# Re-ordering a spline convolution layer: all distances of a turn first, the copies of the next turns earlier, the output add between the splines, and the last stores on two queues

## The chip, the core and the metric

The kernel runs on one core of a Trainium2 chip. A core has four compute engines[...]: TensorE (PE, matrix multiplications; PEld is its weight load), VectorE (DVE), ScalarE (ACT) and GpSimd (POOL). SyncE (SP) only issues DMAs here. Everything is fp32. Time is the device time of one execution in microseconds (us).

## The reference, cut to what matters

Four convolution layers run one after the other on x of shape (8 images, 16 channels, 128, 128), each as x = x + layer(group norm(x)). The change touches the last one, a layer of cubic B-splines:

```python
patches = _extract_patches(x, KSIZE, STRIDE, PAD)          # 3x3 neighbours of each point
bspl = _b_splines(patches, grid)                           # 8 spline values of each element
base_w = base_weight.sum(axis=2)
spl_w = (spline_weight * spline_scaler[..., None]).sum(axis=2)
out = jnp.einsum('bjhwn,ijn->bihw', jax.nn.silu(patches), base_w)
out = out + jnp.einsum('bjhwns,ijns->bihw', bspl, spl_w)
out = out + bias_weight[None, :, None, None]
...
x = x + _L3_conv_ref(_gn(x), ...)
```

So every element becomes eight spline values, these are convolved 3x3 down to 16 channels, a 3x3 convolution of silu(x) is added, then a bias and x itself.

## The kernel before

The stage is laid out in 32 **turns**. A turn (k, g) makes output rows 8k to 8k+7 of four images, those numbered 2q+g with q from 0 to 3; g alternates, so two turns in a row share k. x stays in SBUF, one partition for each image and channel. In the text, "image q" of a turn is the q-th of its four.

The splines of a turn, class `Splines`, take these steps. Its rows are split into two halves, h = 0 and 1, of four rows each (512 columns)[...].

- `spread(h)`: TensorE copies the 16 channels of each image onto 128 partitions (eight spline bases by 16 channels) by a matrix of zeros and ones, four PSUM tiles `far`, one an image (L1204). An fp32 matrix multiplication shows as two instructions in the trace. The pool holds six `far` tiles, so a spread needs two that the spread just before it used.
- `near(h, q)`: ScalarE turns one `far` tile into the scaled distance from the base's centre, `v` (L1149, `v<-far`). The tile `v` has four buffers and 1024 columns, both halves of one image.
- `clip(q)`: VectorE limits `v` to 6 (L1154) and the tiles `e` and `p`, two buffers each, are taken.
- `finish(q)`: ScalarE makes `e` and `p` from `v` (L1149, `e<-v` and `p<-v`), VectorE multiplies them into `p` (L1162, "the p step") and writes the spline values to a tile `s` (L1169, `put`, "the spline"). GpSimd copies the two rows that overlap from the `s` of two turns earlier (L1258). The twelve `s` tiles hold three turns.

The last two turns have seven new rows (896 columns) in place of eight. The first row of an image, `first_row`, is made apart, in the two first turns.

`convolve(t, lo, hi)` adds positions lo to hi-1 of fifteen to the accumulator `acc3` of turn t (L1322): twelve positions of splines and three of silu, each with four products (one for each image, in its own 32 columns of the array), eight instructions a position in the trace. `acc3` has two buffers.

`finish(t)` outside the class adds accumulator, bias and the residual (the tile `o`, L1335, four buffers), and stores it with eight DMAs. `residual(t)` loads `o` with eight DMAs from x (L1301). `silu(k)` serves two turns: ScalarE makes `sil` (one buffer, its edges set to zero by GpSimd at L1269 and L1270), and sixteen DMAs spread it to `four` (L1286, two buffers).

The order of work on VectorE, ScalarE and TensorE is the order of the calls: `in_turn` ties each instruction to the one before it on its engine. GpSimd and SyncE are ordered by a scheduler, roughly as the calls stand. Every buffer is guarded by semaphores that the framework places. Each DMA of SyncE also waits for the landing of the one eight places before it.

`make(t, conv, done)` is the turn: it makes the splines of turn `t` while turn `conv`, two before it, is convolved, and the output of turn `done`, one before `conv`, is finished. The lines of the profile lie in the functions below.

Of the kernel before, what the change touches and what calls it, by code (L numbers as in the profile page):

```python
# [21 lines left out]
NP = B // 2  # L22
# [78 lines left out]
def kernel(  # L101
# [20 lines left out]
    nc = tc.nc  # L122
# [22 lines left out]
    def lut(out_, in_, func, **kw):  # L145
        name = sets.get(func, str(func))
        last = phase["all"]
        if name != phase["name"]:
            phase.update(name=name, first=None, all=[])
            if name == "exp_ln":  # L150
                begin(nc.scalar.preload_act_table_set("natural_log_exp_and_others").ins, last)
        ins = nc.scalar.activation(out_, in_, func, **kw).ins  # L152
        if phase["first"] is None:
            begin(ins, last)
        else:
            tc.add_manual_dep(ins, phase["first"].name, order, reason="table set")
        phase["all"].append(ins)
        return ins
# [51 lines left out]
    def in_turn(engine, ins):  # L210

        if engine in chain:
            tc.add_manual_dep(ins, chain[engine].name, order, reason="in turn")
        chain[engine] = ins
        return ins
# [3 lines left out]
    for n in range(5):  # L219
        t = cpool.tile([BC, BC], F32, name=f"w1_{n}")  # L220
# [13 lines left out]
    with ExitStack() as l0:  # L234
        wp = l0.enter_context(tc.tile_pool(name="w0", bufs=1))
        with tc.tile_pool(name="x0", bufs=2) as xp:
            bn0 = xp.tile([BC, NCH, 6], F32, name="bn0", bufs=1)
            for j in range(8):
                t = xp.tile([BC, HW // 8], F32, name="xj")
# [102 lines left out]
        def work(name):  # L342
            return tmp.tile([128, 2, 512], F32, tag="work", name=name, bufs=11)
# [28 lines left out]
        class Variances:  # L372
# [19 lines left out]
            def finish(self):  # L392
                w, pv = work("r0"), banks[:, 0]
                r0, sq = w[:, 0], w[:, 1]
                lut(r0, pv, AF.Ln, bias=eps_t, scale=-2.0)
                lut(r0, r0, AF.Exp, scale=-0.5)
                nc.scalar.activation(sq, r0, AF.Square)
                nc.vector.scalar_tensor_tensor(pv, pv, -0.5 * EPS, sq, op0=ALU.add, op1=ALU.mult)
                r = act.tile([128, 512], F32, name="rstd", bufs=2)
                nc.vector.scalar_tensor_tensor(r, pv, 1.5, r0, op0=ALU.add, op1=ALU.mult)  # L400
                return r
# [254 lines left out]
        for n in range(-2, NCH + 3):  # L656
            if n + 2 < NCH:
                steps[n + 2] = Step(4 * (n + 2))
            done = steps.pop(n - 2, None)
# [6 lines left out]
            def put(i, f, *a):  # L666
                between[i].append(lambda: f(*a))
# [458 lines left out]
    with ExitStack() as l3:  # L1126
# [24 lines left out]
        def curve(v, width):  # L1151

            v = v[:, :width]
            in_turn("dve3", nc.vector.tensor_scalar_min(v, v, 6.0).ins)  # L1154
            e = tmp.tile([128, 1024], F32, name="e")[:, :width]
            p = tmp.tile([128, 1024], F32, name="p")[:, :width]
            yield
            act(e, v, AF.Square, scale=1.0 / 3.0, bias=minus)
            act(p, v, AF.Prelu, scale=1.0 / 3.0, bias=minus, alpha=-3.0)
            in_turn(  # L1160
                "dve3",
                nc.vector.scalar_tensor_tensor(  # L1162
                    p, p, 3.0, e, op0=ALU.subtract, op1=ALU.mult
                ).ins,
            )
            yield v, p
# [8 lines left out]
        turns = [(k, g) for k in range(H // 8) for g in range(2)]  # L1175
# [14 lines left out]
        def of(t, q):  # L1190
            return tiles[4 * (t % 3) + q]
# [4 lines left out]
        def spread_rows(t, lo, n):  # L1196

            g = turns[t][1]
            out_ = []
            for q in range(NP):  # L1200
                p = ps.tile([128, 512], F32, name="far", bufs=6)
                in_turn(
                    "pe3",
                    mm(  # L1204
                        p[:, : n * W],
                        copy[32 * q : 32 * q + 32, g],
                        x[32 * q : 32 * q + 32, lo * W : (lo + n) * W],
                        start=True,
                        stop=True,
                    ).ins,  # L1210
                )
                out_.append(p[:, : n * W])
            return out_

        def distance(v, p, t, q):
            b = 2 * q + turns[t][1]
            act(v, p, AF.Abs, scale=fac[:, 0, b : b + 1], bias=fac[:, 1, b : b + 1])

        def first_row(t):
            ps_ = spread_rows(t, 0, 1)  # L1220
            v = tmp.tile([128, 1024], F32, name="v", bufs=4)
            for q, p in enumerate(ps_):
                distance(v[:, q * W : (q + 1) * W], p, t, q)
            c = curve(v, 512)
            next(c)
            v, p = next(c)
            for q in range(NP):
                cols = bass.ts(q, W)
                put(of(t, q)[:, 1, 1 : 1 + W], v[:, cols], p[:, cols])
                nc.gpsimd.tensor_copy(of(t, q)[:, 0, :], edge)  # L1230
# [77 lines left out]
        def convolve(t, lo, hi):  # L1308

            k, g = turns[t]  # L1310
            if lo == 0:
                accs[t] = ps.tile([128, 4, W], F32, name="acc3")
            for n in range(lo, hi):
                s, dw = divmod(n, 3)
                for q in range(NP):
                    if s < 4:
                        w_, v = wspl[:, s, dw], of(t, q)[:, s : s + 7 : 2, dw : dw + W]
                    else:
                        w_, v = wbase[:, g, dw], sils[k][:, q, :, dw : dw + W]
                    in_turn(  # L1320
                        "pe3",
                        mm(  # L1322
                            accs[t][32 * q : 32 * q + 32],
                            w_.rearrange("p a f -> p (a f)"),
                            v,
                            start=(n == 0),
                            stop=(n == 14),
                            skip_group_check=True,
                        ).ins,
                    )  # L1330

        def finish(t):
            k, g = turns[t]
            o = outs.pop(t)
            ins = nc.vector.scalar_tensor_tensor(  # L1335
                o, accs.pop(t), bias3, o, op0=ALU.add, op1=ALU.add
            ).ins
            in_turn("dve3", ins)
            for q in range(NP):
                for p in range(2):  # L1340
                    lo = 32 * q + 16 * p
                    nc.sync.dma_start(
                        out[2 * q + g, :, 8 * k : 8 * k + 8, :].rearrange(
                            "f (i p) w -> f p i w", p=2
                        )[:, p],
                        o[lo : lo + 16],
                    )

        def make(t, conv, done):

            sp = Splines(t) if t < len(turns) else None
            if conv is not None:
                convolve(conv, 0, 2)
            if sp:
                if sp.k == 0:
                    first_row(t)
                sp.spread(0)
                for q in range(NP):
                    sp.near(0, q)
            if conv is not None:  # L1360
                convolve(conv, 2, 7)
            if sp:
                sp.spread(1)
                sp.near(1, 0)
                sp.clip(0)
                sp.near(1, 1)
                sp.clip(1)
                sp.finish(0)
                sp.near(1, 2)
                sp.clip(2)  # L1370
                sp.finish(1)
            if conv is not None:
                convolve(conv, 7, 15)
            if done is not None:
                finish(done)
            if sp:
                sp.near(1, 3)
                sp.clip(3)
                sp.finish(2)
                sp.finish(3)  # L1380

        silu(0)
        make(0, None, None)
        residual(0)
        make(1, None, None)
        for t in range(len(turns)):
            if t + 1 < len(turns):
                residual(t + 1)
            if t % 2 == 0 and t + 2 < len(turns):
                silu(t // 2 + 1)  # L1390
            make(t + 2, t, t - 1 if t else None)
        finish(len(turns) - 1)


# [71 lines left out]
```

## Time and profile before

| what | us |
|---|---|
| median of 3 runs | 11252.07 (11250.59 to 11255.03) |
| the profiled execution | 11250.13 |
| its span, first to last instruction | 11248.3 |
| the stage concerned, from the first `sil` memset | 10569.6 to 11248.3 |
| time from one turn's output add to the next, in the middle of the stage | 20.47 |
| one distance, 128x512 (ScalarE L1149) | 0.773 |
| one `e` and one `p`, 128x1024 (ScalarE L1149) | 1.146 and 1.137 |
| one p step and one spline, 128x1024 (VectorE L1162, L1169) | 1.220 and 1.225 |
| one limit, 128x1024 (VectorE L1154) | 0.689 |
| one output add, 128x512 (VectorE L1335) | 0.745 |
| one `sil`, 128x1280 (ScalarE L152) | 1.442 |

The profile is of one execution. A group of instructions is shown as line, engine, operation, tile written <- tiles read, shape and count, then busy time and mean, then the idle time of the engine just before them and what ended it. In the lines of waits, "A <- B" means that A's engine stood idle until B; the numbers are the total, the count and the longest. PEclk is the share of TensorE's full clock that was granted. Durations of two neighbouring instructions on one engine overlap a little, so the time from start to start is shorter than a duration.

Around this stage, the turns before the first convolution take from 10,578 to about 10,619 us, and the convolutions end at 11,241.6.

### The profile page before, as it was taken

The page shows a single profiled execution, that of the slowest core. Times are in us where ns is not written, and L with a number is a line of the kernel's source. Part 1 is how long each engine was busy: PE and PEld are TensorE (multiplying, and loading weights), DVE is VectorE, ACT ScalarE, POOL GpSimd, SP SyncE. Part 2 cuts the span into 40 slices and gives each one's busy share as a digit, 9 for nine tenths or more (in the row PEclk, how much of TensorE's full clock was granted, in tenths as well). Part 3 has the DMA queues.
Part 4 walks back from the last instruction along what each step waited for, and adds up shares of the span by engine and source line. Part 5 has one row for each costly group of instructions (what it writes and reads, how often), then busy time and mean ns, then how long its engine had stood idle before and what let it go on. Part 6 is the DMA issues. An engine that isn't in the chain of part 4 may idle for free.

```text
span 11248.3 us, 173864 instructions
## 1 busy us (share of the span) xinstructions
PE 8843.7 (79%) x72372; PEld 2092.2 (19%) x72372; DVE 9068.7 (81%) x6829; ACT 8780.2 (78%) x7107; POOL 4873.1 (43%) x2681
## 2 busy tenths in 40 slices
PE   5999999999986777777777777777777777777788
PEld 1222222222222111111111111111111111111122
DVE  3555555555555799999999999999999999999865
ACT  2555555555545799999999999999999999999876
POOL 3555555555553633333334333334334333343300
PEclk8999999999998899999999999999999999999899
DMA  1000000000003300000000000000000000000022
GB/s 47 13 15 15 12 13 15 15 13 13 14 6 94 119 7 7 13 7 7 8 12 7 7 13 7 7 13 7 7 13 7 7 13 7 7 7 7 20 54 50
DMA packets 189391, 203.91 MB, mean 18 GB/s; under 512 B 46777, under 2 KB 155449, under 8 KB 186553
## 3 DMA queue, kind: packets, MB, share of 16 engines
q1 hardware_dynamic: 180264, 190.81, 6.4%
q8 instruction: 569, 9.32, 0.3%
q10 hardware_dynamic: 8336, 1.97, 0.1%
q14 instruction: 222, 1.81, 0.1%
HBM read 107.15 MB, written 60.04 MB: 15 GB/s over the span
## 4 chain that ended last, share of the span: by engine, by line
DVE 44%; PE 31%; ACT 14%; issue 5%; POOL 2%; DMA 1%; SPq 1%; DVEq 0%; ACTq 0%; POOLq 0%
DVE t L1003 22%; PE banks L360 17%; DVE u L1009 14%; PE pn L971 10%; ACT t L992 9%; DVE y L518 2%; PE acc L1322 2%; ACT u L152 1%; POOL y L527 1%; DVE x L538 1%; ACT hid L152 1%; PE pd L971 1%; DMA yd<-y 1%; DVE x L630 1%; SPq L1286 1%
## 5 line engine op out<-in xcount | busy, mean ns | idle before, releaser
L971 PE MATMUL pn<-f,wa 32*64 32x512 f32 x18432 | 3413.7, 625 | 1711.6 <-DVE u L1009 1687.3
L1024 POOL TENSOR_TENSOR v<-t,u 128x1024 f32<-128x1024 f32 x1152 | 2739.8, 2378 | 4017.4 <-DVE t L1003 3871.3
L1009 DVE TENSOR_TENSOR u<-pn,u 128x1024 f32<-128x1024 f32 x2304 | 2713.7, 1219 | 117.7
L971 PE MATMUL pd<-f,wb 32*64 32x512 f32 x18432 | 2601.0, 626 | 161.1 <-ACT t L992 94.6
L1003 DVE SCALAR_TENSOR_TENSOR t<-t,u 128x2048 f32<-128x2048 f32 x1152 | 2630.6, 2283 | 33.9 <-ACT u L152 33.6
L992 ACT ACTIVATE t<-pd 128x1024 f32<-128x1024 f32 x2304 | 2338.4, 1015 | 311.2 <-PE pn L971 304.7
L152 ACT ACTIVATE u<-t 128x2048 f32<-128x2048 f32 x1152 | 2202.5, 1912 | 51.9 <-PE acc L1055 15.9
L152 ACT ACTIVATE u<-u 128x2048 f32<-128x2048 f32 x1152 | 2190.7, 1902 | 0.0
L971 PEld LDWEIGHTS pn<-f,wa 32*64 32x64 f32 x18432 | 750.0, 131 | 3775.4 <-DVE u L1009 3246.1
L1016 DVE SCALAR_TENSOR_TENSOR u<-t,u 128x1024 f32<-128x1024 f32 x1152 | 1418.5, 1231 | 37.9
L152 ACT ACTIVATE hid<-banks 128x1024 f32<-128x1024 f32 x576 | 571.8, 1023 | 1049.6 <-PE banks L360 1047.7
L1055 PE MATMUL acc<-u,const 128*32 128x512 f32 x9216 | 1257.2, 618 | 1.8 <-DVE u L1016 1.8
L527 POOL TENSOR_TENSOR y<-y 128x1536 f32<-128x1536 f32 x256 | 895.0, 3496 | 833.6 <-DVE y L518 833.6
L518 DVE TENSOR_TENSOR y<-banks,vp 128x1536 f32<-128x1536 f32 x384 | 673.0, 1753 | 274.8 <-PE banks L360 271.6
L544 ACT ACTIVATE sq<-x 128x1024 f32<-128x1024 f32 x384 | 398.0, 1054 | 412.3 <-DVE x L538 289.7
L470 POOL TENSOR_TENSOR pd<-q,kp 128x1536 f32<-128x1536 f32 (+1 forms) x256 | 694.0, 2737 | 7.6 <-PE banks L360 5.9
L971 PEld LDWEIGHTS pd<-f,wb 32*64 32x64 f32 x18432 | 514.5, 132 | 751.9 <-ACT t L992 690.7
L360 PE MATMUL banks<-att,const 32*128 32x512 f32 x2304 | 499.0, 669 | 173.7 <-DVE att L509 96.0
L360 PE MATMUL banks<-h,wfc 64*128 64x512 f32 (+1 forms) x3072 | 620.5, 632 | 14.5 <-DVE h L606 14.5
L1055 PE MATMUL acc<-v,const 128*32 128x512 f32 x4608 | 616.5, 606 | 0.2 <-POOL v L1024 0.2
L606 DVE TENSOR_TENSOR h<-banks,x 128x1024 f32<-128x1024 f32 x192 | 232.6, 1211 | 437.9 <-ACT hid L152 227.6
L1322 PE MATMUL acc<-s,wspl 128*32 128x512 f32 x3072 | 389.2, 650 | 92.5 <-DVE o L1335 92.5
(181 smaller groups left out, 7329.3 us busy)
## 6 DMA issues: line engine op xcount, KB each, us to landing
f<-yd SPq DMA_DIRECT2D x512, 101.6 KB
yd<-y SPq DMA_DIRECT2D x320, 130.0 KB
xin<-in_x SPq DMA_DIRECT2D x752, 32.0 KB
four<-sil SPq DMA_DIRECT2D x256, 65.0 KB
xj<-in_x SPq DMA_DIRECT2D x8, 1024.0 KB
xl<-in_x SPq DMA_DIRECT2D x32, 256.0 KB
x1d<-xl SPq DMA_DIRECT2D x32, 256.0 KB
x<-x1d SPq DMA_DIRECT2D x8, 1024.0 KB
```

The source lines that it names most:

```text
L152: ins = nc.scalar.activation(out_, in_, func, **kw).ins
L360: in_turn("pe", mm(*args, skip_group_check=True, **kw).ins)
L470: ins = nc.gpsimd.tensor_mul(t[:, :n].rearrange("p n (a b) -> p n a b", a=4), rows(self.q[d][:, k]).unsqueeze(1).to_broadcast([128, n, 4, W]),
L518: ins = nc.vector.tensor_mul(y.rearrange("p n (a b) -> p n a b", a=4), banks[:, 1:4].rearrange("p n (a b) -> p n a b", a=4), windows(v, j, 3),
L527: in_turn("pool", nc.gpsimd.tensor_add(self.y[k], self.y[k], y).ins)
L971: yield mm(p[64 * (u % 2) : 64 * (u % 2) + 64, u // 2], w[lo : lo + 32, q % 2, n].rearrange("p c f -> p (c f)"), fs[g * NP + q][lo : lo + ...
L992: in_turn("act", nc.scalar.activation(self.t[:, ab], self.pd.pop(ab), AF.Abs).ins)
L1003: ins = nc.vector.scalar_tensor_tensor(self.t, self.t, 1.0, self.u, op0=ALU.add, op1=ALU.mult).ins
L1009: ins = nc.vector.tensor_mul(self.u[:, ab], self.pn.pop(ab), self.u[:, ab]).ins
L1016: ins = nc.vector.scalar_tensor_tensor(r, self.t[:, :, 0], 2.0, r, op0=ALU.subtract, op1=ALU.mult).ins
L1024: ins = nc.gpsimd.tensor_mul(self.v, self.t[:, :, 1], self.u[:, :, 1]).ins
L1055: ins = mm(accs[k][32 * q : 32 * q + 32], gather[:, int(part == 1), g], (c.u[:, ab, 0], c.u[:, ab, 1], c.v[:, ab])[part], start=first, sto ...
```

## The change

`make` is split. `begin_turn(t)` starts the splines of a turn: the first row if there is one, `spread(0)` and `near(0, q)` of all four images. `make(sp, done)` then issues all second halves of the distances with their limits, and after them the four `finish(q)`, with the output add of turn `done` between images 1 and 2. `done` is now the turn just convolved, t, where it was t-1. The loop places the two spreads of turn t+2 after eight and after ten of the fifteen positions of turn t (before: after two and after seven). Turn 0 has an order of its own, since the splines of turn 1 are still being made in it. In the last turn, every second image's two stores are issued from ScalarE in place of SyncE.

```diff
             for q in range(NP):
+
+                eng = nc.scalar if t == len(turns) - 1 and q % 2 else nc.sync
                 for p in range(2):
                     lo = 32 * q + 16 * p
-                    nc.sync.dma_start(
+                    eng.dma_start(
...
-        def make(t, conv, done):
-
-            sp = Splines(t) if t < len(turns) else None
-            if conv is not None:
-                convolve(conv, 0, 2)
+        def begin_turn(t):
+
+            if t >= len(turns):
+                return None
+            sp = Splines(t)
+            if sp.k == 0:
+                first_row(t)
+            sp.spread(0)
+            for q in range(NP):
+                sp.near(0, q)
+            return sp
+
+        def make(sp, done):
+
             if sp:
-                if sp.k == 0:
-                    first_row(t)
-                sp.spread(0)
                 for q in range(NP):
-                    sp.near(0, q)
-            if conv is not None:
-                convolve(conv, 2, 7)
-            if sp:
-                sp.spread(1)
-                sp.near(1, 0)
-                sp.clip(0)
-                sp.near(1, 1)
-                sp.clip(1)
-                sp.finish(0)
-                sp.near(1, 2)
-                sp.clip(2)
-                sp.finish(1)
-            if conv is not None:
-                convolve(conv, 7, 15)
-            if done is not None:
+                    sp.near(1, q)
+                    sp.clip(q)
+                for q in range(NP):
+                    if q == 2 and done is not None:
+                        finish(done)
+                    sp.finish(q)
+            elif done is not None:
                 finish(done)
-            if sp:
-                sp.near(1, 3)
-                sp.clip(3)
-                sp.finish(2)
-                sp.finish(3)
 
         silu(0)
-        make(0, None, None)
+        sp = begin_turn(0)
+        sp.spread(1)
+        make(sp, None)
+        sp = begin_turn(1)
         residual(0)
-        make(1, None, None)
         for t in range(len(turns)):
             if t + 1 < len(turns):
                 residual(t + 1)
             if t % 2 == 0 and t + 2 < len(turns):
                 silu(t // 2 + 1)
-            make(t + 2, t, t - 1 if t else None)
-        finish(len(turns) - 1)
+            if t == 0:
+                convolve(t, 0, 2)
+                sp.spread(1)
+                make(sp, None)
+                convolve(t, 2, 8)
+            else:
+                convolve(t, 0, 8)
+            sp = begin_turn(t + 2)
+            convolve(t, 8, 10)
+            if sp:
+                sp.spread(1)
+            convolve(t, 10, 15)
+            make(sp, t)
```

## The prediction

> **What bounds the kernel now.** The edit lies in the last stage alone (span 10,569 to 11,248 us), so I read only that. First the waits of a stretch of ten turns there (10,900 to 11,104 us, 20.48 us a turn):
>
> ```profile
> POOL s L1258 <- PE acc L1322: 151.2, 10, 19.0
> DVE v L1154 <- ACT v L1149: 56.4, 10, 5.7
> ACT v L1149 <- PE far L1204: 40.8, 20, 2.7
> PE acc L1322 <- DVE o L1335: 32.4, 10, 3.2
> ```
>
> Columns: total us, times, longest. POOL's wait delays nobody; the other three form a ring. TensorE cannot open a turn until VectorE's `o` of the turn before has freed an accumulator (3.2 us each), ScalarE waits for TensorE's copies, VectorE for ScalarE. No engine is full. What each would need alone comes from the groups of the same stretch:
>
> ```profile
> L1169 DVE SCALAR_TENSOR_TENSOR s<-v,p 128x1024 f32<-128x1024 f32 x40 | 49.0, 1225 | 4.7
> L1162 DVE SCALAR_TENSOR_TENSOR p<-p,e 128x1024 f32<-128x1024 f32 x40 | 48.8, 1220 | 15.9 <-ACT p L1149 15.9
> L1154 DVE TENSOR_SCALAR v<-v 128x1024 f32<-128x1024 f32 x40 | 27.3, 689 | 56.4 <-ACT v L1149 56.4
> ...
> L1149 ACT ACTIVATE e<-v,minus 128x1024 f32<-128x1024 f32 x40 | 45.8, 1146 | 16.1 <-DVE v L1154 15.1
> ```
>
> VectorE: 49.0+48.8+27.3+7.5 (`o`) = 132.6 for ten turns, 13.3 a turn. ScalarE: 57.6+45.8+45.5+7.2 = 156.1, 15.6 by durations; starts overlap ends, so by start-to-start (0.67 a copy, 1.05 an `e` or `p`, 1.34 a `sil` every second turn) it is 8x0.67+8x1.05+0.67 = 14.4. Next, the granted clock in three stretches, the columns after the stretch being its length and the engines' busy times:
>
> ```profile
> 10971.88:10975.29 3.41, 3.41 (x16) 0.68 (x16) 3.31 (x4) 2.98 (x3) 0.00 (x0) 0.50 0.27 57
> 10975.29:10992.36 17.07, 13.84 (x128) 3.86 (x128) 9.46 (x11) 12.49 (x15) 1.68 (x6) 1.00 0.34 74
> 10992.36:10995.77 3.41, 3.41 (x16) 0.64 (x16) 3.31 (x4) 2.19 (x2) 0.00 (x0) 0.50 0.27 58
> ```
>
> After each stop for `o`, TensorE runs 3.41 us at half clock. Warm, four convolution instructions start every 0.431 us, so a turn's 120 take 12.93, its two `far` groups 1.07 each: 15.07 us. Last, the timeline of SyncE's DMA queue for two turns:
>
> ```profile
> 11012.65 3.64 SPq L1342 DMA_DIRECT2D out<-o  x8
> 11016.86 10.67 SPq L1286 DMA_DIRECT2D four<-sil  x16
> 11027.58 1.88 SPq L1301 DMA_DIRECT2D o<-x  x3
> 11033.12 3.63 SPq L1342 DMA_DIRECT2D out<-o  x8
> 11036.80 9.17 SPq L1301 DMA_DIRECT2D o<-x  x13
> ```
>
> 28.99 us in two turns of 40.96: idle for 12.
>
> [...] ScalarE idles 1.5 us for `e` ten times although the `sil` behind needs nothing of it. So an order of issue is an order of execution, and I may add start-to-start times. [...] at 10,591.15 the `p` step took 1.43 beside a GpSimd copy, against 1.22. [...]
>
> **The change, part by part.** Per engine the instructions stay the same; they are re-ordered, and four of 256 store DMAs go to ScalarE's queue.
>
> *Output add.* `finish(t)` moves from turn t+1 into turn t's own splines, behind image 1's. Accumulators are two, so turn t+1 needs the one that t-1 freed a turn earlier. TensorE's 3.24 us stop goes, and with it the cold window (16 instructions in 3.41 us instead of 1.72, so 1.7). What is late next? With TensorE free, 15.07 would be the turn, if nothing else were longer.
>
> *All distances first.* ScalarE's order is now near(0,0..3), near(1,0..3), then e, p for images 0 to 3. `v` has four buffers, one for each image, so near(0,3) of the next turn must wait for image 3's spline, the last VectorE step of this one, and all eight remaining distances and curves stand behind it. That closes a new ring. With near(0,3) at 0, from start-to-start times of the timeline: near(1,0) 0.67, near(1,3) 2.70, e0 3.36, p0 4.41, first `p` step 5.57 (1.16 after p0). VectorE then runs unbroken: four pairs of `p` step to spline (1.34), after images 0, 1 and 2 1.14, after `o` 0.66: 4x1.34+3x1.14+0.66 = 9.44 (the 1.14 behind image 1 leads to `o`, at 10.5), so image 3's spline starts at 15.01, lasts 1.23, and near(0,3) follows 0.04 later: **16.28 us**. Does anything inside wait longer? e and p have two buffers: e2 needs the first `p` step done (6.84, its turn 7.56), p3 needs spline 1 (10.66, its turn 10.71): no. `sil` runs 11.72 to 13.06, before near(0,3): hidden by this wait; without that cover it would cost 0.67 a turn.
>
> *Copies ahead.* spread(0) of turn t+2 goes behind 8 of 15 positions, spread(1) behind 10. The second one's images 2 and 3 wait for near(0,0) and near(0,1), at the latest 14.5; conv(t,10..15) and the next 8 positions are queued behind. They end 5 and 12 us later, `o` needs the first at 10.5 of the next round (26.8), so 7 us of slack. TensorE idles 1.2 us a turn here on average, 2.6 in a `sil` turn and none in the next. Should that turn it cold, 1.7 is lost against those 2.5 per pair of turns: still hidden.
>
> *Queues passed.* SyncE's blocks keep their order per pair: 8 stores, 16 `four`, 3 loads, 8 stores, 13 loads: 29 of now 32.6 us. A round's stores start at 11.3, `four` at 15.1, lands by 29, wanted by the memset and `sil` at 44.3. GpSimd's four copies (0.36 each) wait for a convolution that ends near 2.3 to 3.6 and are over by 5.1, before VectorE's two-input steps at 5.57; bound 0 to 1.4 us a turn, I take 0.
>
> *Prologue.* Turn 0: e0 moves from 10,585.92 to 10,587.1 behind four distances, but the curves then run unbroken: splines end 10,599.0 (before 10,599.5). Turn 1: its first row at 10,600.6, `sil`, near(1,0) 10,604.8, p0 10,608.5, last spline done 10,619.4 (before 10,618.8): +0.6.
>
> *End.* 28 rounds of 16.28 and one of 14.6 (the last two turns have 896 columns: 0.67+1.71+0.57+0.95+1.06, then 4x1.2+3x1.01+0.66, then 1.13): 10,619.4+455.8+14.6 = 11,089.8. Turn 31's last spline is done 14.6 later, 11,104.4; conv(30) ends about 11,104.6; conv(31) 12.93+0.5: 11,118.0. `o` 0.75. From there to the end before: 5.9 us, with eight issues of 0.46; two queues halve them, -1.8 (bounds 0 and -1.8): 11,122.9.
>
> **Sum.** I add 0.1 us a round for waits taken as exact: 11,125.8 span. The profiled execution took 11,250.13 for a span of 11,248.3, so 1.83 around it: 11,127.6. The median of the runs is 1.94 above that execution: 11,129.5, rounded **11,130 us**, 1.1% less. About 0.2%, 22 us, is what a measurement can tell from no change.
>
> **Rivals.**
> A (forecast): the `v` ring, 16.3 to 16.5: 11,122 to 11,140. Chance 0.72.
> B: a round of 17 to 17.8. The turn of before is exactly six clock windows (20.48); if TensorE's idle falls into one window it may settle at five, 17.07: 0.69x29 = 20 over the forecast's 16.38, 11,150. Or SyncE's DMAs, spaced by landings, stretch as traffic grows by a quarter: 29 to 35 per pair, the same figures. For: 2.6 of 3.41 us idle can be cold. Against: the slack above. 0.17.
> C: TensorE's own 15.07, if near(0,3)'s wait came earlier than I read: -1.3x29: 11,092. Against: `v` has four buffers in both kernels. 0.07.
> D, slower: `four`'s landing. `sil` stands ahead of all distances on ScalarE and waits for the last turn-pair's sixteen DMAs and a GpSimd memset; if they land more than 16 us (44.3-28.2) late, ScalarE stops, and with it VectorE, TensorE and the next stores. Past a round of 20.48 it loses: landing 16+8.3 = 24 us late per pair. A round of 22.5 would give 11,250+2x29 = 11,310. Nothing in the queue shows such a delay. 0.03.
> E: the stage is bound by something I do not see and stays: 11,250. 0.01.
> So faster 0.96, same 0.01, slower 0.03; range 11,110 to 11,160, which leaves out C, the upper part of B, and D.
>
> **What would show it.** Right: turns 16.3 apart; "PE acc <- DVE o" gone; ScalarE's L1149 `v` waiting some 1.1 to 2.5 us per turn for DVE `s` L1169; clock near 1.00 in the stage; SyncE idle about 3 us per pair; TensorE's waits moved to `far` <- ACT `v`. Wrong: turns of 17 us or more with SyncE never idle or a 0.50 clock each turn (B); 15.1 us with no ACT wait on DVE `s` (C); ACT `sil` waiting for DMA `four` (D).

## The result, and the profile after

| | before | after |
|---|---|---|
| median (range), us | 11251.33 (11248.15 to 11255.03), 4 runs | 11132.26 (11130.52 to 11134.61), 4 runs |
| ratio to before | | 0.9894, 95% interval 0.9881 to 0.9907 |
| span of the profiled execution | 11248.3 | 11132.8 |
| last stage, from its first distance to the end of the span | 669.9 | 551.1 |
| one output add to the next, mean over the middle of the stage | 20.35 | 16.45 |
| last output add (its start) to the end of the span | 6.72 | 5.36 |
| time at half clock from 10,625 us to the end of the span | 95.5 | 12.9 |

The kernel became 119 us, 1.1%, faster; the forecast was 11,130 us, 1.1%. In the profiled executions the last stage is 118.8 us shorter, and what runs ahead of it took 3.3 us longer. (A round is the time from one turn's output add to the next.) Some 29 rounds shorter by 3.90 make 113, the shorter end 1.4; the remaining 4 lie in the first and last turns.

The waits of ten turns of the kernel after come first (total us, times, longest us):

```profile
DVE v L1154 <- ACT v L1149: 16.0, 10, 1.6
DVE p L1162 <- ACT p L1149: 13.8, 10, 1.4
ACT v L1149 <- DVE s L1169: 13.6, 11, 1.9
...
PEld far L1204 <- ACT v L1149: 11.0, 14, 1.5
ACT v L1149 <- PE far L1204: 5.2, 4, 1.7
```

TensorE's wait for VectorE's `o` is gone. ScalarE's wait for TensorE has shrunk from 40.8 us to 5.2. A new wait stands in its place: ScalarE, about to make a `v`, waits for VectorE's spline. ScalarE's timeline shows where in a turn (start, us, engine, line; in brackets the idle time before):

```profile
10866.64 0.78 ACT L1149 ACTIVATE v<-far,fac 128x512 f32<-128x512 f32 x1 [0.64 <-DVE s L1169]
10869.32 3.46 ACT L1149 ACTIVATE v<-far,fac 128x512 f32<-128x512 f32 x5 [1.90 <-DVE s L1169]
...
10881.00 1.44 ACT L152 ACTIVATE sil<-x,d,rs 128x1280 f32<-128x1280 f32 x1
10882.34 2.10 ACT L1149 ACTIVATE v<-far,fac 128x512 f32<-128x512 f32 x3
10885.62 3.46 ACT L1149 ACTIVATE v<-far,fac 128x512 f32<-128x512 f32 x5 [1.18 <-DVE s L1169]
```

The group of five is near(0,3) with the four distances near(1,0..3) behind it. In both turns it starts only when image 3's spline has freed a `v`; in the second turn `sil` fills part of the same wait. In two of the ten turns the waits are put down to TensorE's copies (5.2 us above), but near(0,3) starts there some 0.12 us after the spline's end, as in the others.

The next views are of some twenty turns: one stretch (bounds, length, busy time with instructions of PE, PEld, DVE, ACT, POOL, then granted clock, DMA share, GB/s), and two groups of it.

```profile
10696.00:11022.00 326.00, 322.68 (x2696) 90.26 (x2692) 258.33 (x259) 287.77 (x328) 70.84 (x100) 0.98 0.31 66
```

```profile
L1162 DVE SCALAR_TENSOR_TENSOR p<-p,e 128x1024 f32<-128x1024 f32 x79 | 98.1, 1242 | 26.2 <-ACT p L1149 26.2
...
L1258 POOL COPY s<-s 128x260 f32<-128x260 f32 x80 | 69.5, 884 | 143.3 <-DVE s L1169 107.4 <-PE acc L1322 27.2 <-PE far L1204 8.4
```

The clock is 0.98 on average; in the kernel before, a stretch at 0.50 followed 27 of the 29 stops for `o`. GpSimd's copies, 442 ns each in the kernel before, take 884 ns and are now released mostly by a spline instead of by TensorE: they run beside VectorE. SyncE's queue, over 460 us (14 pairs of turns), waits for `o` 52.1 us, 3.7 a pair:

```profile
SPq L1344 <- DVE o L1335: 52.1, 15, 12.3
```

### The profile page after: what moved, and what is told of

Its sections match the earlier page's. It is cut to its first block, busy times and chain, and to the rows that moved or that the text cites. A ratio compares the mean times of both kernels' runs of the same rounds, so it can differ in the third digit from the quotient of the medians.

```text
span 11132.8 us, 173994 instructions
## 1 busy us (share of the span) xinstructions
PE 8824.5 (79%) x72372; PEld 2092.4 (19%) x72372; DVE 9078.7 (82%) x6829; ACT 8772.0 (79%) x7107; POOL 4922.7 (44%) x2681
## 3 DMA queue, kind: packets, MB, share of 16 engines
q14 instruction: 221, 1.81, 0.1%
## 4 chain that ended last, share of the span: by engine, by line
DVE 45%; PE 31%; ACT 14%; issue 5%; POOL 2%; DMA 1%; SPq 1%; DVEq 0%; ACTq 0%; POOLq 0%
DVE t L1003 22%; PE banks L360 18%; DVE u L1009 14%; PE pn L971 10%; ACT t L992 9%; DVE y L518 2%; PE acc L1322 1%; POOL y L527 1%; DVE x L538 1%; PE pd L971 1%; ACT hid L152 1%; ACT u L152 1%; DMA yd<-y 1%; DVE x L630 1%; DVE p L1162 1%
## 5 line engine op out<-in xcount | busy, mean ns | idle before, releaser
L360 PE MATMUL banks<-rstd,const 32*128 32x512 f32 (+1 forms) x1216 | 411.5, 641 | 19.4 <-DVE rstd L400 15.1
```

What stands on the lines that cost most here:

```text
L360: in_turn("pe", mm(*args, skip_group_check=True, **kw).ins)
```

## The experiments

All are told by three figures: the median with its ratio to the kernel before, which ran beside each; the mean round in the middle of the stage; and the stage, from its first distance to the end of the span, which leaves out the variation of the earlier stages. The kernel after has 16.45 and 551.1.

### Five buffers for `v`

```diff
-        v = tmp.tile([128, 1024], F32, name="v", bufs=4)
+        v = tmp.tile([128, 1024], F32, name="v", bufs=5)
```

The same is done at the other two places that take a `v`.

> The changed kernel with five buffers for the distances v instead of four. My theory, the v ring: a round of the changed kernel (16.41 us, from one output add to the next) is set by near(0,3) waiting for the last spline of the turn before. With a fifth buffer it waits for the spline of image 2 only, which is 2.5 us earlier; the ring then allows 13.8, and TensorE's own 15.07 us becomes the turn: 15.1 to 15.3, so 29 x 1.2 = 35 us less than the changed kernel, about 11,097. Rival 1, the e and p buffers (two each) hold ScalarE: no change, 16.4 a round. Rival 2, SyncE's DMAs set the turn (29.1 us of work in a pair of 32.8): no change, or half of it.

Measured: 11097.33 us (0.9866, interval 0.9851 to 0.988), round 15.35, stage 523.0. The waits of ten turns in this kernel:

```profile
DVE p L1162 <- ACT p L1149: 12.7, 10, 1.4
...
ACT v L1149 <- PE far L1204: 6.6, 5, 1.3
DVE v L1154 <- ACT v L1149: 6.2, 10, 0.7
```

ScalarE's `v` no longer waits for the spline; what it still waits for, every second turn, is TensorE. One `v` buffer more takes 1.1 us from every round, so the ring through `v` is shown. TensorE's timeline tells what bounds now:

```profile
10863.56 1.14 PE L1204 MATMUL far<-x,const 32*128 32x512 f32 x8
10864.64 1.93 PE L1322 MATMUL acc<-s,wspl 128*32 128x512 f32 x16
10866.50 1.14 PE L1204 MATMUL far<-x,const 32*128 32x512 f32 x8
10867.57 1.93 PE L1322 MATMUL acc<-s,wspl 128*32 128x512 f32 x16
10869.31 2.77 PE L1322 MATMUL acc<-four,wbase 128*32 128x512 f32 x24
10871.90 7.09 PE L1322 MATMUL acc<-s,wspl 128*32 128x512 f32 x64
10878.92 1.14 PE L1204 MATMUL far<-x,const 32*128 32x512 f32 x8
```

From the first `far` to the one a turn later is 15.36 us without an idle bracket. Sixteen convolution instructions take 1.74 from start to next start where more convolution follows, and 1.86 where a `far` follows; sixty-four with a `far` behind them take 7.02, against 64/4 x 0.431 = 6.90. Each change from convolution to copies so costs about 0.12 us, twice a turn: that is nearly the whole distance from the forecast's 15.07 for TensorE alone to 15.35.

### Three buffers for `e` and `p`

```diff
-            e = tmp.tile([128, 1024], F32, name="e")[:, :width]
-            p = tmp.tile([128, 1024], F32, name="p")[:, :width]
+            e = tmp.tile([128, 1024], F32, name="e", bufs=3)[:, :width]
+            p = tmp.tile([128, 1024], F32, name="p", bufs=3)[:, :width]
```

> The changed kernel with three buffers for e and for p instead of two, v at four. The v ring: p3 needs spline 1 at 10.66 of the round and its turn comes at 10.71, so a third buffer relieves a wait of nothing: 16.4 us a round, 11,132, within 3 us. Rival, the e and p buffers are what holds ScalarE: the round shortens towards 15.1, about 11,095.

Measured: 11132.19 us (0.9897, 0.9882 to 0.9912), round 16.44, stage 551.0: nothing. These buffers hold nobody up, as the working of the prediction had it.

### The copies ahead put back

```diff
-            else:
-                convolve(t, 0, 8)
-            sp = begin_turn(t + 2)
-            convolve(t, 8, 10)
...
-            convolve(t, 10, 15)
+            else:
+                convolve(t, 0, 2)
+                sp = begin_turn(t + 2)
+                convolve(t, 2, 7)
+                if sp:
+                    sp.spread(1)
+                convolve(t, 7, 15)
```

Turn 0 keeps the order of the kernel after.

> The changed kernel with the two spreads of turn t+2 put back behind two and behind seven of the fifteen positions, as before the change (turn 0 keeps its own order). My theory: where TensorE does its copies costs nothing so long as they land before near(0,0) and after the far buffers are free. The far tiles of the second spread still wait for near(0,1), so eight positions instead of five stand behind that wait: the convolution then ends 2.6 us later, at about 5 us of a round whose output add comes at 10.5. So 16.4 us a round, 11,132 within 4. Rival: the place of the copies is a good part of the gain; then a round of 17 to 18.5, 11,150 to 11,195.

Measured: 11137.91 us (0.9902, 0.9887 to 0.9916), round 16.50, stage 554.9. By the stage it is 3.8 us longer, 0.05 a round and some 2 at the end; by the medians 5.7, a little more than was expected. Where the copies stand hardly matters, as long as the round is set by `v`.

### The output add behind all four splines

```diff
                 for q in range(NP):
-                    if q == 2 and done is not None:
-                        finish(done)
                     sp.finish(q)
-            elif done is not None:
+            if done is not None:
                 finish(done)
```

> The changed kernel with the output add of turn t behind the spline of image 3 instead of between images 1 and 2. My theory: between the images the add lies inside the ring and costs it 0.66 us (its start to the next start); behind image 3 it falls into VectorE's wait for the next distances. 15.7 us a round, 29 x 0.7 = 20 us less: about 11,112. The accumulator is then free at 16.3 of the round, and turn t+2 wants it at about 17.5: just in time. Rival: it is too late, TensorE stops for it again as in the kernel before, and goes cold: 17 us or more, over 11,150.

Measured: 11116.49 us (0.9882, 0.9865 to 0.9898), round 15.78, stage 534.6. The add's own 0.66 us leaves the ring, because image 3's spline, and so the next near(0,3), comes that much earlier.

### The output add of the turn before, in the new order

The distances come first, but the add stays a turn late.

```diff
-            make(sp, t)
+            make(sp, t - 1 if t else None)
+        finish(len(turns) - 1)
```

> The changed kernel with the output add of turn t-1, not t, between images 1 and 2 (the last one behind everything): the other parts of the change alone. My theory: the accumulator for turn t+1 then comes free at 11.3 of the round, and behind it stand eight positions, cold (8.6 us), and the spread that near(0,0) waits for; near(0,3) follows at about 23. So a turn of 23, slower than the kernel before: about 11,330. Rival: the distances first are the gain and the add is a detail: 16.4 to 18, 11,130 to 11,180.

Measured: 11344.24 us (1.0086, 1.0069 to 1.0103), round 23.89, stage 768.0, slower than the kernel before. Its waits over ten turns:

```profile
DVE v L1154 <- ACT v L1149: 91.4, 10, 9.2
ACT v L1149 <- PE far L1204: 91.3, 10, 9.8
PE acc L1322 <- DVE o L1335: 63.5, 10, 6.4
```

This is the old ring, made longer. In the new order the add stands behind eight distances and all the limits; TensorE waits for it 6.4 us a turn (3.2 in the kernel before), and 197 us of the span run at half clock after 10,625 us (95.5 in the kernel before). Distances first does not pay without the moved add; it costs 3.5 us a round.

### The output add early, in the old order

The kernel before, with the add moved from behind image 1's spline to ahead of image 0's second distance. It is still the add of the turn before.

```diff
                 sp.spread(1)
+                if done is not None:
+                    finish(done)
                 sp.near(1, 0)
...
-            if done is not None:
+            if not sp and done is not None:
                 finish(done)
```

> The kernel before, with one part of the change alone: the output add of turn t-1 stands ahead of the second halves of turn t+2's distances instead of behind the spline of image 1, so the accumulator is free some 10 us sooner; order of distances and place of the copies as before. My theory: TensorE's stop for the add (3.24 us a turn) and the half clock after it go, and a ring between ScalarE and TensorE is next: near(0,0) to near(1,0) 5.5 us (a spread and five positions between them), from there to the end of the curves 12.2, a sil of 1.34 every second turn: 18.4 a turn instead of 20.47, 11,190 or so. That is half of the gain, and the order of the distances has the other half. Rival: the add alone has nearly all of it, 16.5 to 17 a turn, about 11,140.

Measured: 11121.09 us (0.9887, 0.9872 to 0.9902), round 15.91, stage 542.5. Both expectations were too slow. The theory took the stretch from near(0,0) to near(1,0), 5.5 us in the kernel before, as part of a ring; it was only TensorE being late with its copies. Freed of its stop, TensorE runs so far ahead that the copies lie ready: these are all the waits of ScalarE in ten turns, and TensorE is not among them (40.8 us in the kernel before).

```profile
ACT e L1149 <- DVE v L1154: 8.0, 10, 0.8
ACT v L1149 <- DVE s L1169: 4.2, 5, 0.8
```

So this one move has more than the whole gain of the change: its stage is 8.6 us shorter than that of the kernel after.

### The last stores on one queue

```diff
-                eng = nc.scalar if t == len(turns) - 1 and q % 2 else nc.sync
+                eng = nc.sync
```

> The changed kernel with all stores of the last turn on SyncE's queue. Read at its end, from the start of the last output add to the end of the span: 6.7 us in the kernel before, 5.4 in the changed one. My theory: 6.7 again, for four more issues of 0.46 on one queue. Rival: the landing sets it and the second queue does nothing: 5.4.

Measured in one run: 11136.83 us, round 16.43, last add to end 6.72, as in the kernel before. The queues' own lines (start, us, queue, line), first of this kernel, then of the kernel after:

```profile
11129.10 3.63 SPq L1344 DMA_DIRECT2D out<-o  x8
```

```profile
11128.25 1.81 ACTq L1344 DMA_DIRECT2D out<-o  x4
```

```profile
11128.25 1.73 SPq L1344 DMA_DIRECT2D out<-o  x4
```

The eight issues take 3.63 us on one queue and 1.81 on two. Of the 1.82 saved, 1.36 to 1.49 arrive at the end of the span (6.72 against 5.36 in the kernel after and 5.23 to 5.33 in the others with two queues). What the second queue saves here is time of issue.

### Without GpSimd's copies

```diff
+        for t in tiles[8:]:
+            nc.gpsimd.memset(t[:, 0:2, 1 : 1 + W], 0.0)
...
-                if self.k:
-                    nc.gpsimd.tensor_copy(t[:, 0:2, :], of(self.t - 2, q)[:, 8:10, :])
```

> The changed kernel without GpSimd's copies of the two overlapping rows (L1258), so the top two rows of each tile of splines are stale; four tiles are zeroed once. In the changed kernel rounds of 16.29 and 16.51 alternate. My theory: the 0.22 is a p step of VectorE (1.42 instead of 1.22)[...]. Without the copies every round is 16.29, 0.11 less on average, about 3 us in all. Rival: it comes from the sil of every second round: the alternation stays.

Measured in one run: 11114.21 us, 16.00 in every round, stage 539.6. Both expectations were off: the alternation went, but the gain is four times the theory's 0.11. The kernel after alternates between 16.29 and 16.52, so the copies cost 0.44 a round on average, in both kinds of round. VectorE's timeline in the kernel after, the end of a long round:

```profile
10863.97 1.22 DVE L1162 SCALAR_TENSOR_TENSOR p<-p,e 128x1024 f32<-128x1024 f32 x1
10865.29 1.23 DVE L1169 SCALAR_TENSOR_TENSOR s<-v,p 128x1024 f32<-128x1024 f32 x1
10866.45 1.42 DVE L1162 SCALAR_TENSOR_TENSOR p<-p,e 128x1024 f32<-128x1024 f32 x1
10867.97 1.23 DVE L1169 SCALAR_TENSOR_TENSOR s<-v,p 128x1024 f32<-128x1024 f32 x1
```

And the same two steps without the copies:

```profile
10865.41 1.21 DVE L1162 SCALAR_TENSOR_TENSOR p<-p,e 128x1024 f32<-128x1024 f32 x1
10866.65 1.23 DVE L1169 SCALAR_TENSOR_TENSOR s<-v,p 128x1024 f32<-128x1024 f32 x1
10867.80 1.22 DVE L1162 SCALAR_TENSOR_TENSOR p<-p,e 128x1024 f32<-128x1024 f32 x1
10869.05 1.23 DVE L1169 SCALAR_TENSOR_TENSOR s<-v,p 128x1024 f32<-128x1024 f32 x1
```

There are two costs. From p step to spline is 1.32 with copies and 1.24 to 1.26 without, four times a round. It is there in rounds in which no copy runs beside that pair, and in the kernel before too, so a copy running at the same moment does not account for it; what does was not shown. The other cost falls on every second round: one p step takes 1.42, and its spline starts 1.52 after it. GpSimd's timeline of the kernel after shows a copy train there:

```profile
10864.61 0.12 POOL L1269 MEMSET sil<- 128x10 f32 x1 [11.38 <-DMA o<-x]
...
10864.74 3.39 POOL L1258 COPY s<-s 128x260 f32<-128x260 f32 x3
```

GpSimd is held up by the memset of the edges of `sil`, behind which three copies pile up and then run beside VectorE's steps, in 3.39 us together. The long round is the one that ends with this train; `sil` itself runs on ScalarE in the next one, at 10,881.00. The p step that begins during this train takes 1.42, against 1.22 for the others shown. The copies are 0.88 on average, against 0.44 in the kernel before: in the next round the two that begin during a p step (10,877.57 and 10,883.16) take 1.27 each, the two that do not (10,880.04 and 10,885.63) 0.40.

### Five `v` buffers and the add last

The edits of two experiments above, together.

> The kernel after with five buffers for v, and the output add behind all four splines instead of between those of images 1 and 2. Each of the two alone shortened the round: 15.35 us (five buffers) and 15.78 (add last), from 16.45. Theory: with five buffers TensorE is already the bound (its work stands back to back, 15.36 us a turn), so the add's 0.66 us on VectorE no longer counts: round 15.3 to 15.4, time 11,093 to 11,100, within 5 us of five buffers alone. Rival: VectorE's chain still holds up part of the round with five buffers, and TensorE only looks full because its instructions stretch over what they wait for: then the round goes to 15.1 and the time to 11,090.

Measured: 11101.43 us (0.987, 0.9855 to 0.9885), round 15.35, stage 523.3. The stage is that of five buffers alone to 0.3 us. With five buffers the 0.66 us of the add cost nothing, so VectorE is off the path and TensorE bounds, as the theory said.

### Early add, five `v` buffers, two queues, in the old order

The kernel before with the early add, `bufs=5` at its three places for `v`, and

```diff
+                eng = nc.scalar if t == len(turns) - 1 and q % 2 else nc.sync
...
-                    nc.sync.dma_start(
+                    eng.dma_start(
```

> The kernel before with three edits: the output add moved ahead of image 0's second distance (15.9 us a round when done alone), v with five buffers, the last stores on two queues. Theory: v's ring of four buffers is what held that order at 15.9, as it did the kernel after; with five TensorE bounds it as well: round 15.3 to 15.5, time 11,097 to 11,104, so the order of the distances was worth nothing. Rival: in that order ScalarE waits for VectorE inside the turn (clips between the distances), not for a v buffer: the round stays 15.8 to 15.9, and only the end moves, -1.4: 11,118 to 11,121.

Measured: 11117.29 us (0.9883, 0.9866 to 0.9899), stage 537.0, rounds of 16.10 and 15.31 in turn. Each expectation holds for half of the rounds: the turns without `sil` come down to TensorE's pace, those with it do not. ScalarE in a turn with `sil`:

```profile
10869.96 1.15 ACT L1149 ACTIVATE e<-v,minus 128x1024 f32<-128x1024 f32 x1 [0.79 <-DVE v L1154]
10871.02 1.14 ACT L1149 ACTIVATE p<-v,minus 128x1024 f32<-128x1024 f32 x1
10872.06 1.44 ACT L152 ACTIVATE sil<-x,d,rs 128x1280 f32<-128x1280 f32 x1
10873.41 4.10 ACT L1149 ACTIVATE v<-far,fac 128x512 f32<-128x512 f32 x6
```

From image 0's `e` of this turn to that of the next is 16.11 us, and ScalarE is idle for only 0.79 of it, waiting for image 3's limit. With `sil` in the turn ScalarE has no other idle time. Distances first takes that wait away and lets ScalarE work ahead over two turns: mean 15.35 instead of 15.74. That is what the new order is worth once `v` no longer binds; the copies ahead and the place of the add differ too and were not separated from it here.

## Why the prediction was right, point by point

- **The ring through `v`.** Forecast 16.28 a round, with 0.1 added 16.38; measured 16.45. That it is this ring is shown by five buffers and by ScalarE's 1.18 to 2.54 us of waiting a turn for the spline (forecast 1.1 to 2.5). In short rounds without disturbance the time is 16.29 to 16.30, within 0.02 of the sum, in part by luck: after near(0,3) at 10,869.32 image 3's spline starts at 14.95 where 15.01 was forecast, and the next near(0,3) follows its end by 0.12 where 0.04 was. Each start in between held to 0.06.
- **GpSimd's copies: the step that failed.** The prediction let them run early in the round and end by 5.1 us, and took 0. They follow the splines, and cost 0.44. Only 0.11 of that shows as an error, because the rest, the longer way from p step to spline, was already in the pitch of 1.34 read from the kernel before. The 0.1 added for waits taken as exact covered most of it, by luck and not by reason.
- **The output add.** The stop for `o` and the cold window behind it went as forecast. That such a window costs the 1.7 us forecast, the kernel before shows itself: the turn after one stop had none, and took 18.78 where its neighbours took 20.27 to 20.38 (last section). The prediction had the add's 0.66 in its sum of the ring; what it did not ask is whether a move of the add alone would bring the whole gain, as it does, and whether a place outside the ring would save the 0.66, as it does too.
- **The copies ahead** were costed at nothing, hidden by the ring: putting them back costs 0.05 a round, so that was right. A cold window was to stay hidden as well: the one at 10,884.96 lies in a stretch from one near(0,3) to the next of 16.52 us, as long as others of its kind.
- **The order of ScalarE's work** was right for the time but its worth was not asked. With four buffers it closes the `v` ring. With the add inside that ring the round is 16.45, longer than the 15.91 of the old order with an early add; with the add behind all splines it is 15.78, about even; with a fifth buffer 15.35 stand against 15.74. (Of the prediction's ten waits for `e`, `sil` stands behind five, not behind all.)
- **Prologue.** Round 0's near(0,3) came 0.3 us later than forecast, once the 3.3 us of the earlier stages are taken off.
- **End.** The next-to-last convolution was to end with the last spline; the last convolution could begin only 2.3 us after that spline's end. At 11,096.94, when TensorE had made its last copies, 160 instructions of the next-to-last convolution still lay before it, and it ran them without a gap. The two queues were priced at -1.8 and gave 1.36 in the kernel after.
- **The sum.** For the stage the forecast was 547.3 us (11,125.8 less its start at 10,578.5), the measurement 551.1. The 3.8 missing are, rounding aside, 1.3 in 28 rounds, 0.3 in the prologue, 2.1 in the next-to-last convolution and 0.5 in the end, less 0.3 in the last turns.
- **The rivals.** B fell: SyncE idles 3.7 us a pair, and only three windows in the turns were cold. C is what the kernel does with a fifth buffer, at 15.35 and not 15.07; most of the difference is the 0.12 us at each of the two changes from convolution to copies, missing from its sum. D did not show: no `sil` waits for `four`.

The fastest version tried is the kernel after with five buffers for `v`: 11097.33 us, a stage of 523.0 against 551.1 and 669.9. Its turns are TensorE's instructions back to back.

## What to carry to other kernels

Where an engine's order puts all first steps of the next round ahead of the rest, count the buffers of what these steps write: with exactly one for each unit of a round, the last of them waits for the last unit of the round before, and everything behind it does too; one more buffer opened that ring. Look first for the small step that frees the bottleneck engine's buffer, here an add of 0.75 us, and put it early, but outside the chain that sets the round; then test each part of a bundle alone, since here a move of the add alone brought more than the whole gain, and the new order without it was a loss. When a ring is opened, sum the next engine's instructions from start to start, with the changes between kinds of work in it.

## What the runs showed of the hardware that was not expected

- In the kernel with five buffers, going from the convolution (128 rows by 32 columns) to the copies (32 by 128) cost TensorE about 0.12 us each time. What takes this time was not shown. The weight loads (PEld) differ too: there they take 0.18 us on average for the copies and 0.11 for the convolution.
- TensorE lost its clock after stretches in which it was not idle throughout. In the traces of the kernel before and the kernel after, the changes of the clock in the turns lie whole multiples of 3.413 us apart, to within 1 ns, so each trace can be cut into windows of that length. In the kernel after, a window in which TensorE only slowed down, the first line, was followed by one at 0.50 (columns as in the stretch above):

```profile
10881.54:10884.96 3.42, 3.06 (x16) 0.97 (x16) 3.21 (x4) 2.90 (x4) 1.27 (x1) 1.00 0.35 75
10884.96:10888.37 3.41, 3.41 (x20) 0.87 (x24) 1.81 (x3) 2.75 (x5) 0.40 (x1) 0.50 0.32 70
```

In the kernel after it happened in only three of the turns, 99 us or six turns apart, though the same gap recurs in every second turn. How a gap falls on the windows made the difference for one stop of the kernel before. It lasted 3.24 us like the others, from 10,847.82 to 10,851.06, but fell across two windows, and neither these nor the next was cold:

```profile
10845.59:10849.00 3.41, 2.23 (x24) 0.42 (x16) 3.17 (x4) 3.41 (x5) 0.00 (x0) 1.00 0.00 0
10849.00:10852.41 3.41, 1.35 (x16) 0.50 (x16) 3.39 (x4) 1.90 (x2) 0.00 (x0) 1.00 0.09 19
10852.41:10855.83 3.42, 3.42 (x36) 0.94 (x32) 3.21 (x4) 3.42 (x5) 0.00 (x0) 1.00 0.24 49
```

The counts in these lines take in instructions that only reach into a window. By the instructions that start in it, the line for 10,881.54 has 12, and the first two lines for the kernel before have 16 each; a window of convolution has about 31. Over the turns of these two traces, from 10,640 us to 60 us before the end, the warm windows with at most 10 starts were all followed by a cold one (23 of 23), those with 11 or 12 in 6 of 10 cases, and those with 16 or more never (none of 224); none had 13 to 15. So about a third of a window's work, 10 of some 31 starts, did not keep the clock here.
